# Expert rows gathered by token number, radial layers on parts of the TensorE array, and the last 226 counts summed in SBUF

## The chip, the cores and the metric

The kernel runs on one core of a Trainium2 chip. The metric is the device time of that core in microseconds (us), one launch from begin to end, lower is better. The engines are named as the profile names them: PE (TensorE, the matrix engine), DVE (VectorE), ACT (ScalarE), POOL (GpSimd), SP (SyncE, which here only issues DMAs). PSUM, where PE writes, has eight banks of 512 fp32 columns.

## The reference, cut to what matters

The input `x` has 1250 rows of 512. Four blocks follow one another, each added to its own input:

```python
x = x + gnn(layernorm(x), edge_attr_4, edge_attr_8, edges)   # 40000 edges, dst is sorted
x = x + grouped_moe(layernorm(x))
x = x + gat2(layernorm(x), edges)                            # two attention layers, 4 heads x 256, and a linear
x = x + expert_choice(layernorm(x))                          # 16 experts
```

The change touches the first two:

```python
# gnn: x0 = up-projected scalars (n,128), x1 = vectors (n,128,3)
h = edge_feats                                   # (edges, 8)
for W in (W1, W2, W3):                           # 8x64, 64x64, 64x64
    h = c * silu(h @ W / sqrt(len(W)))
w1, w2, w3, w4 = split(h @ W4 / 8, 4)            # 64 -> 4 x 128
p1 = w1 * x0[src] * y0;      p2 = w2 * x0[src] * y1
p3 = w3 * x1[src] * y0;      p4 = w4 * sum(x1[src] * y1) / sqrt(3)
msg = segment_sum(p1, p4, p2, p3 by dst);  out = lin(msg) / 10

# grouped_moe: 4 groups of 8 experts, every token keeps 2 groups, and in each of them 2 experts
gw = topk_gate(x @ wg_group, 2);  z = layernorm(x)
for g: iw = topk_gate(z @ wg_inner[g], 2)
       y_g = layernorm(z + sum_e iw[e] * (relu(z @ W1[g,e] + b1) @ W2[g,e] + b2))
out = sum_g gw[g] * y_g
```

The attention layers need the same edges as a dense matrix of counts, 1250 by 1250: how many edges go from one node to another. It is made together with the segment sums of the first block.

## The kernel before, in words

**Stages.** By the trace, the first 87 us project `x` up to `xup_d` and order the edges; the edge stage runs from there to 735 us; a block stage (735 to 898) projects the sums out and gates the tokens; the 32 experts run from 898 to 1141; their rows are brought back and combined until 1240; the attention layers follow to about 1980 and the expert-choice block to the end.

**The edge stage** (`edge_sums`, from L464) walks over 45 steps. A step takes 4 columns (`CG`) x 2 halves (`GT`) x 128 edges. Its order is written out by hand in `beat(s)`: in one beat different steps are in different phases, and each engine runs its instructions in that order. In beat s, SP loads the edges of step s+4 (L516), DVE makes the indices of step s+3 (L521), POOL gathers the sender rows of step s+2 by eight indirect DMAs of 128 rows of 3300 bytes each (L528: 2 KB of scalars and vectors, then the sender's one-hot row of 1250 in fp8, from which the counts come), PE and ACT run the radial network of step s+2, weights and products are made for step s+1, and the sums are taken for step s.

PE's order in a beat: layer 0 (L545, four products of 128 columns each, with a `w1` that is mostly zeros), the weights of pair 0 (L581; a pair is one half of the edges in two columns, and its two products use 64 rows of the array each), part of the sums (L613, L620, four 32-column tiles side by side), layer 1 (L548, one product of 512 columns with a block-diagonal 128x128 `w2`, two 64x64 blocks on the diagonal and zeros elsewhere), sums, weights of pair 1, the counts of half 0 (L630: fp8, 1250 columns as 512 + 512 + 226, four columns of edges each), layer 2 (L548), weights of pair 2, sums, a transpose (L95), weights of pair 3, sums, the counts of half 1. ACT does the silus (L553), copies each pair's weights from PSUM to SBUF (L588, two copies a pair), copies sums and counts out (L640, L646) and scales what stays in PSUM for the next step (L643, L647: by 1 where a window of nodes goes on, by 0 where not; `going`). DVE multiplies weights and rows (L597 twice and L600 for each of four pairs), makes the one-hot matrices (L561, L564, L569), and in steps 4 to 27 also runs one of 24 slices of products for the attention layers (`att_products`, L1936). POOL also stores each step's 128 rows of 2274 fp32 to `sums_d` (L650, an indirect DMA). SP in addition writes zeros into `zs_d`, two blocks of 128 rows a step (issued in `side`, 88 DMAs of 256 KB).

The PSUM tiles are `pa` (sums, two banks), `pc` (counts, three), `pw` (weights, two buffers of one bank) and `pm` (layers, one). Node windows that need more than 45 steps, which no input of this shape here needs, lie behind an If.

**Grouped experts** (`grouped_moe`, from L836). Five blocks of two chunks of 125 tokens each: load the sums (`acc`) and project them out, layer norm, gating, a running count of tokens for each expert, and from it the slot of each of a token's four (expert, token) pairs. Each expert has 208 slots in `zs_d`. POOL adds the norm's bias to the row `z` (L1008), and eight indirect DMAs a block (L1043) write the 125 rows of 2 KB of a chunk to their slots, 40 in all; a pair beyond an expert's 208 slots goes to overflow tiles, which are behind an If that isn't taken with this input. SP's queue loads `acc` and `adj` rows and the first experts' weights; ACT's queue stores what becomes of `adj`. The order in this stage is made by a scheduler. Then each expert (L1132ff): SP loads its 208 rows as `zr` in one DMA of 416 KB, PE transposes them (L95) and multiplies with W1 and W2 (L1150, L1159), ACT applies relu (L1152), DVE adds the row (L1161), and ACT's queue stores `y` over the expert's slots. At the end the four rows of each token are gathered by `pair_slot` (L1215), and combined (L1256).

Of the kernel before, what the change touches and what calls it, by code (L numbers as in the profile page):

```python
# [53 lines left out]
MOE_ROWS = 32 * MOE_SL + MOE_NT * MOE_TS  # L54
# [406 lines left out]
def edge_sums(k, tables, sorted_d, xup_d, Ws, sums_d, zero, side):  # L461
# [14 lines left out]
    with ExitStack() as es:  # L476
# [7 lines left out]

        HC = CG // 2
        w1 = cp.tile([128, TT // 2, 128], F32, name="w1")
        nc.gpsimd.memset(w1, 0.0)
        w2 = cp.tile([128, 128], F32, name="w2")
        nc.gpsimd.memset(w2, 0.0)
        w3 = cp.tile([128, 128], F32, name="w3")  # L490
        nc.gpsimd.memset(w3, 0.0)
        w4 = cp.tile([128, 4 * 128], F32, name="w4")
        for u in range(2):
            half = slice(u * 64, (u + 1) * 64)
            for t in range(GT):
                for jp in range(HC):
                    r = ((2 * jp + u) * GT + t) * PW + 4
                    nc.sync.dma_start(w1[r:r + 8, t * HC + jp, half], Ws[0])
            nc.sync.dma_start(w2[half, half], Ws[1])
            nc.sync.dma_start(w3[half, half], Ws[2])  # L500
            nc.sync.dma_start(w4[half, :], Ws[3])
# [4 lines left out]
        pc = ps_a.tile([128, 3 * 512], F32, name="pc")  # L506
# [25 lines left out]
        def turn(s):  # L532
            pm = nets[s] = ps_m.tile([128, 512], F32, name="pm")
            k.transpose(pm[:, :128], pays[s].rearrange("p j t w -> p (j t w)"))

        def features(s):
            f = ep.tile([128, 128], F32, name="f")
            nc.scalar.copy(f, nets[s][:, :128])
            nets[s] = f

        def layer(s, i):
            pm = ps_m.tile([128, 512], F32, name="pm")
            if i == 0:
                for b in range(TT // 2):
                    nc.tensor.matmul(pm[:, b * 128:(b + 1) * 128], w1[:, b, :], nets[s], start=True,  # L545
                                     stop=True)
            else:
                nc.tensor.matmul(pm, (w2, w3)[i - 1], nets[s], start=True, stop=True)  # L548
            nets[s] = pm

        def silu(s, i):
            h = ep.tile([128, 512], F32, name=f"h{i}", bufs=1 + i // 2)
            nc.scalar.activation(h, nets[s], AF.Silu,  # L553
# [21 lines left out]
        def weights(s, t, jp):  # L575
            b = t * HC + jp
# [47 lines left out]

        def counts(s, t):
            eq = hots[s][0]
            for o in range(0, N, 512):
                e = min(N, o + 512)
                for j in range(CG):
                    nc.tensor.matmul(pc[j * WIN:(j + 1) * WIN, o:e], eq[:, j * GT + t, :],  # L630
                                     rows[s, t, j // 2][:, j % 2, D:].bitcast(FP8)[:, o:e],
                                     start=s == t == 0, stop=t == GT - 1, skip_group_check=True,
                                     tile_position=(0, j * WIN))
# [4 lines left out]
        def take_sums(s):  # L638
            outs[s] = ep.tile([128, SUMS], F32, name="out", bufs=3)
# [5 lines left out]
        def take_counts(s):  # L645
            nc.scalar.copy(outs[s][:, 1024:], pc[:, :N])  # L646
            nc.scalar.activation(pc[:, :N], pc[:, :N], AF.Copy, scale=going[:, s:s + 1])  # L647

        def store(s):
            st = nc.gpsimd.indirect_dma_start(  # L650
                out=sums_d, out_offset=bass.IndirectOffsetOnAxis(ap=sum_rows[:, s:s + 1], axis=0),
                in_=outs.pop(s), in_offset=None, bounds_check=CARRY + 127, oob_is_err=False)
# [14 lines left out]
        def carry_counts(s):  # L667
            if s == NS0 - 1:
                for o in range(0, N, 512):
                    e = min(N, o + 512)  # L670
                    nc.tensor.matmul(pc[:, o:e], carry_to, outs["carry"][:, 1024 + o:1024 + e],
                                     start=False, stop=True, skip_group_check=True)

# [13 lines left out]
        def beat(s):  # L687
# [31 lines left out]
            do(0, counts, 0)  # L719
            do(2, gather, 1)  # L720
# [12 lines left out]
            do(1, products, *pairs[3])  # L733
            do(0, sums, 1, 0, 3)
# [15 lines left out]
        with tc.If(rarely > 0):  # L750
            for s in range(NS0, NS):
# [8 lines left out]
                for t in range(GT):  # L760
# [7 lines left out]
                    counts(s, t)  # L768
                take_sums(s)
# [66 lines left out]
def grouped_moe(k, x, sums_d, nb_d, adjT_d, finish, zs_d, W_out0, W_out1, ln_g, ln_b, wg_group, wg_inner,  # L836
                W1, b1, W2, b2, gln_g, gln_b):

# [9 lines left out]
    SL, TS, NT = MOE_SL, MOE_TS, MOE_NT  # L848
# [5 lines left out]
    with ExitStack() as es:  # L854
        mp = es.enter_context(tc.tile_pool(name="moe", bufs=1, reuse_waits="tile"))
        pair_slot = mp.tile([P, NC, 4], I32, name="pair_slot")
        over_slot = mp.tile([P, NC, 4], I32, name="over_slot")
# [13 lines left out]
        teri = mp.tile([1, NT + 1], I32, name="teri")  # L871
        b1T = mp.tile([128, GX * HC], F32, name="b1T")
# [11 lines left out]
        with ExitStack() as s1:  # L884
# [42 lines left out]
            nc.vector.memset(ones, 1.0)  # L927
            ti = tp.tile([NT, 1], F32, name="ti")
# [42 lines left out]
            for blk in range(NB):  # L971
# [18 lines left out]
                for i in range(BC):  # L990
# [17 lines left out]
                    nc.gpsimd.tensor_tensor(z[:, c, :], z[:, c, :], lnb, op=ALU.add)  # L1008
                n = BC * (G + 1)
# [31 lines left out]
                for i in range(BC):  # L1041
                    for j in range(4):
                        st = nc.gpsimd.indirect_dma_start(  # L1043
                            out=zs_d, out_offset=bass.IndirectOffsetOnAxis(ap=p4i[:, i, j:j + 1], axis=0),
                            in_=z[:, blk * BC + i, :], in_offset=None, bounds_check=GX * SL - 1,
                            oob_is_err=False)
# [4 lines left out]
                if blk == 1:  # L1051
                    pre = [load(e) for e in range(6)]

# [36 lines left out]
            nc.vector.tensor_copy(pair_slot, p4)  # L1090
            p4o = tp.tile([P, NC, 4], F32, name="p4o")
            nc.vector.tensor_scalar(p4o, p4, float(GX * SL), FAR, op0=ALU.is_lt, op1=ALU.mult)
            nc.vector.tensor_tensor(p4o, p4o, p4, op=ALU.add)
            nc.vector.tensor_copy(over_slot, p4o)
# [949 lines left out]
```

## Time and profile before

| what | before |
|---|---|
| median of 9 runs | 2253.88 us (2247.28 to 2259.61) |
| the profiled execution | 2251.05 us, span 2249.3 |
| PE busy | 1939.4 us (86%) |
| DVE busy | 1384.9 us (62%) |
| ACT busy | 1023.2 us (45%) |
| POOL busy | 789.7 us (35%) |
| DMA | 421.75 MB, mean 188 GB/s |
| gathers L528 | 360, 433.3 us on POOL |
| `zs_d<-zero` | 88 DMAs of 256 KB |
| `zr<-zs_d` | 32 DMAs of 416 KB |

A busy share is a mean over stages which have different limits, so each stage is read by itself. A group of instructions is shown as line, engine, operation, output<-input, count, then busy time, mean ns of one, and the idle time of the engine just before them with what ended it. On a line of the timeline, the first number is the start in us, the second the duration; "x8" joins eight instructions that follow one another, and brackets hold the idle time before them and what ended it. "issue" is time in which the engine waited for nothing that the profile shows.

### The profile page before, as it was taken

The page shows a single profiled execution, that of the slowest core. Times are in us where ns is not written, and L with a number is a line of the kernel's source. Part 1 is how long each engine was busy: PE and PEld are TensorE (multiplying, and loading weights), DVE is VectorE, ACT ScalarE, POOL GpSimd, SP SyncE. Part 2 cuts the span into 40 slices and gives each one's busy share as a digit, 9 for nine tenths or more (in the row PEclk, how much of TensorE's full clock was granted, in tenths as well). Part 3 has the DMA queues.
Part 4 walks back from the last instruction along what each step waited for, and adds up shares of the span by engine and source line. Part 5 has one row for each costly group of instructions (what it writes and reads, how often), then busy time and mean ns, then how long its engine had stood idle before and what let it go on. Part 6 is the DMA issues. An engine that isn't in the chain of part 4 may idle for free. (4 is left out here: it accounts for less than half of the span.)

```text
span 2249.3 us, 31188 instructions
## 1 busy us (share of the span) xinstructions
PE 1939.4 (86%) x10813; PEld 1111.9 (49%) x10813; DVE 1384.9 (62%) x2944; ACT 1023.2 (45%) x1856; POOL 789.7 (35%) x671
## 2 busy tenths in 40 slices
PE   2599999999998463999979969999999999709996
PEld 2333333333333452766623447885457777505563
DVE  8289999998885455323347399875807777382000
ACT  2277777777775333211125347872216555101221
POOL 3377888887774266100045200000000001002342
PEclk9699999999999665999967989999999999858998
DMA  6799999999995876998644522205211221366752
GB/s 174 229 327 304 331 337 319 338 335 306 312 327 177 248 213 159 288 299 268 213 110 130 135 75 82 57 19 127 77 56 35 76 73 50 91 246 183 225 117 32
DMA packets 196586, 421.75 MB, mean 188 GB/s; under 512 B 66411, under 2 KB 86090, under 8 KB 192818
## 3 DMA queue, kind: packets, MB, share of 16 engines
q0 software_dynamic: 60416, 204.33, 28.8%
q1 hardware_dynamic: 116400, 183.36, 26.9%
q10 hardware_dynamic: 19599, 31.92, 4.5%
q8 instruction: 90, 1.47, 0.3%
q14 instruction: 81, 0.66, 0.1%
HBM read 326.25 MB, written 133.33 MB: 204 GB/s over the span
## 5 line engine op out<-in xcount | busy, mean ns | idle before, releaser
L528 POOL DMA_INDIRECT s<-xup_d,idx x360 | 433.3, 1204 | 130.9 <-issue 82.0
L1553 PE MATMUL po<-h,p 125*125 125x257 f32 x1600 | 363.8, 385 | 20.2 <-ACT p L1546 20.2
L597 DVE TENSOR_TENSOR m<-w,s 128x768 f32<-128x768 f32 x360 | 329.6, 956 | 51.2 <-ACT w L588 49.8
L1553 PEld LDWEIGHTS po<-h,p 125*125 125x125 f32 x1600 | 299.5, 190 | 71.8 <-ACT p L1546 23.1
L588 ACT COPY w<-pw 128x512 f32<-128x512 f32 x360 | 193.3, 589 | 95.1 <-PE pw L581 88.1
L1585 POOL TENSOR_TENSOR xc<-xc,fcb 125x512 f32<-125x512 f32 x10 | 18.2, 1839 | 610.8 <-DMA xc<-x_d 610.7
L1436 PE MATMUL ph<-w,xT 128*125 128x512 f32 x480 | 219.1, 614 | 2.0 <-DMA w<-in_L_gnn_W 0.8
L581 PE MATMUL pw<-w,h 64*128 64x512 f32 x720 | 205.9, 644 | 0.3 <-ACT w L588 0.2
L1532 ACT ACTIVATE q<-rr,ascol 125x250 f32<-125x250 f32 x400 | 165.9, 496 | 60.0 <-DVE p L1534 36.3
L1534 DVE SCALAR_TENSOR_TENSOR p<-rr,acol,q 125x250 f32<-125x250 f32 x400 | 171.0, 477 | 24.2 <-PE po L1553 14.7
L1436 PEld LDWEIGHTS ph<-w,xT 128*125 128x125 f32 x480 | 91.5, 194 | 123.4 <-issue 114.5
L620 PE MATMUL pa<-m,oh 128*32 128x256 f32 x2160 | 143.0, 383 | 0.0
L1488 DVE CUSTOM_DVE_ANT_0 junk<-row,nb 125x1250 bf16<-125x1250 f32 (+1 forms) x80 | 113.2, 1415 | 22.7 <-DMA row<-a_d 16.1
L600 DVE TENSOR_TENSOR m<-w,s 128x512 f32<-128x512 f32 x180 | 122.8, 682 | 0.0
L1538 DVE TENSOR_TENSOR p<-p,adjb 125x1250 f32<-125x1250 f32 x80 | 120.2, 1502 | 1.1
L1546 ACT ACTIVATE p<-p 125x1250 f32<-125x1250 f32 x80 | 98.0, 1240 | 46.5 <-DVE p L1538 34.8
L620 PEld LDWEIGHTS pa<-m,oh 128*32 128x32 f32 x2160 | 61.3, 109 | 117.0 <-issue 93.5
L1882 PE MATMUL po<-w,hT 128*78 128x512 f32 x256 | 115.7, 605 | 0.5 <-ACT hT L1874 0.5
L1159 PE MATMUL po<-w,hT 128*104 128x512 f32 x256 | 115.7, 595 | 0.0
L1161 DVE TENSOR_TENSOR y<-po,zr 104x512 f32<-104x512 f32 x64 | 44.2, 691 | 113.3 <-PE po L1159 111.1
L1152 ACT ACTIVATE hT<-ph,b1T 128x208 f32<-128x208 f32 x64 | 27.8, 434 | 185.0 <-PE ph L1150 171.8
L1827 DVE COPY xg<-px 128x624 f32<-128x624 f32 x16 | 12.9, 806 | 160.0 <-PE px L95 160.0
(461 smaller groups left out, 3100.7 us busy)
## 6 DMA issues: line engine op xcount, KB each, us to landing
w<-in_L_ffn_W SPq DMA_DIRECT2D x64, 512.0 KB
w<-in_L_ffn_w SPq DMA_DIRECT2D x32, 1024.0 KB
zs_d<-zero SPq DMA_DIRECT2D x88, 256.0 KB
zr<-zs_d SPq DMA_DIRECT2D x32, 416.0 KB
zs_d<-y ACTq DMA_DIRECT2D x32, 416.0 KB
adjb<-adjT_d SPq DMA_DIRECT2D x10, 1093.8 KB
rr<-r_d SPq DMA_DIRECT2D x8, 875.0 KB
attw<-in_L_gnn_W SPq DMA_DIRECT2D x12, 512.0 KB
```

The source lines that it names most:

```text
L528: nc.gpsimd.indirect_dma_start(out=sj[:, u], out_offset=None, in_=xup_d, in_offset=bass.IndirectOffsetOnAxis(ap=idxs[s][:, i:i + 1], axis=0))
L581: nc.tensor.matmul(pw, nets[s][half, b * 128:(b + 1) * 128], w4[half, :], start=True, stop=True)
L588: nc.scalar.copy(made[s, t, jp][2][:, u].rearrange("p a d -> p (a d)"), made[s, t, jp][u])
L597: nc.vector.tensor_tensor(m[:, u, :, 1:4, :], w[:, u, 2:4, None, :].to_broadcast(shape), v[:, u, None, 1:4, :].to_broadcast(shape), op=ALU ...
L600: nc.vector.tensor_tensor(m[:, :, :, 0, :], w[:, :, 0:2, :], v[:, :, 0:1, :].to_broadcast([128, 2, 2, 128]), op=ALU.mult)
L620: nc.tensor.matmul(pab[q, 1, a::3 - a, :] if a < 2 else pab[q, 1, 2:4, :], oh[:, i, 1 + a, :], ms[j][:, 1, 0:2 + a:1 + a, :], start=first ...
L1159: nc.tensor.matmul(po[:n], hT[:, hc, j * n:(j + 1) * n], w2[:, hc, :], start=hc == 0, stop=hc == HC - 1)
L1436: self.k.nc.tensor.matmul(ph, self.xT[:, i, c * P:(c + 1) * P], self.w[half][i], start=i == 0, stop=i == kin - 1)
L1532: nc.scalar.activation(q[:, i], rr[:, hd, :, 1, :], AF.Identity, bias=ascol[:, c, hd:hd + 1])
L1534: nc.vector.scalar_tensor_tensor(p[:, i], rr[:, hd, :, 0, :], acol[:, c, hd:hd + 1], q[:, i], op0=ALU.add, op1=ALU.max)
L1538: nc.vector.tensor_tensor(pf, pf, adjb[:, half * HS:(half + 1) * HS, :] .rearrange("p c n -> p (c n)"), op=ALU.add)
L1553: nc.tensor.matmul(po[q], p[:, i, q, :], h[:, c, hd, :], start=c == 0, stop=c == NC - 1)
```

## The change

In the edge stage:

- Layer 0 becomes four products of 64 rows: `w1` keeps both columns' weights of a pair, and rows 0 to 63 and 64 to 127 give different columns of the output. Layers 1 and 2 become four products of 64x64 on the four quarters of the array, 256 columns each; `w2` and `w3` hold two copies of the 64x64 matrix one above the other, with no zeros. The output `pm` has two banks now, of each 256 columns are used, and the halves of a layer's output lie in the order (pair of columns, half of edges).
- The counts' first 1024 columns stay in PSUM as before (`pc`, two banks). The last 226 are multiplied in a `pw` buffer right after the counts of half 0, for both halves (`counts_beyond`), copied by ACT into the step's `out` tile, and summed from step to step there: DVE adds the last step's 226 numbers times `going` (`add_beyond`).
- The zeros of `zs_d` are no longer written.

In the grouped experts:

- The rows `z` are stored once, in the tokens' order, to `z_d` (two SP DMAs a chunk, after L1008's addition). The 40 indirect DMAs now write a token's number (4 bytes) instead of its row to the slots, in a table `tok_d` of 64 x 104 that is filled before with numbers of valid tokens.
- After the last block, the table is loaded to SBUF, transposed by PE and copied by DVE to `token`. Each expert's rows come by two indirect gathers of 104 rows, issued by POOL (64 in all), in place of SP's one load.
- `zs_d` now holds the experts' outputs and the overflow tiles only, and shares its DRAM with `sums_d`. The second slot table `over_slot` is gone; `pair_slot` is worked out with one DVE operation less.

```diff
+        CUT = 1024
+        w1 = cp.tile([128, GT, 128], F32, name="w1")
-        w2 = cp.tile([128, 128], F32, name="w2")
-        nc.gpsimd.memset(w2, 0.0)
+        w2 = cp.tile([128, 64], F32, name="w2")
...
-                    nc.sync.dma_start(w1[r:r + 8, t * HC + jp, half], Ws[0])
-            nc.sync.dma_start(w2[half, half], Ws[1])
+                    nc.sync.dma_start(w1[r:r + 8, t, half], Ws[0])
+            nc.sync.dma_start(w2[half], Ws[1])
...
         def layer(s, i):
-            pm = ps_m.tile([128, 512], F32, name="pm")
-            if i == 0:
-                for b in range(TT // 2):
-                    nc.tensor.matmul(pm[:, b * 128:(b + 1) * 128], w1[:, b, :], nets[s], start=True,
-                                     stop=True)
-            else:
-                nc.tensor.matmul(pm, (w2, w3)[i - 1], nets[s], start=True, stop=True)
+            pm = ps_m.tile([128, 2, 512], F32, name="pm")
+            for b in range(2):
+                for r in range(2):
+                    q = slice(64 * r, 64 * r + 64)
+                    if i == 0:
+                        nc.tensor.matmul(pm[:, r, b * 128:(b + 1) * 128], w1[q, b, :], nets[s][q, :],
+                                         start=True, stop=True)
+                    else:
+                        v = b ^ r
+                        nc.tensor.matmul(pm[64 * v:64 * v + 64, r, :256], (w2, w3)[i - 1][q],
+                                         nets[s][q, 256 * v:256 * v + 256], start=True, stop=True,
+                                         tile_position=(64 * r, 64 * v))
...
+        def counts_beyond(s):
+            pw = ps_w.tile([128, 512], F32, name="pw")
+            for t in range(GT):
+                for j in range(CG):
+                    count(pw, s, t, j, CUT, N, t == 0)
+            outs[s] = ep.tile([128, SUMS], F32, name="out", bufs=3)
+            nc.scalar.copy(outs[s][:, 1024 + CUT:], pw[:, :N - CUT])
+
+        def add_beyond(s):
+            if s > 0:
+                last = outs[s][:, 1024 + CUT:]
+                nc.vector.scalar_tensor_tensor(last, outs[s - 1][:, 1024 + CUT:], going[:, s - 1:s], last,
+                                               op0=ALU.mult, op1=ALU.add)
...
         def take_counts(s):
-            nc.scalar.copy(outs[s][:, 1024:], pc[:, :N])
-            nc.scalar.activation(pc[:, :N], pc[:, :N], AF.Copy, scale=going[:, s:s + 1])
+            nc.scalar.copy(outs[s][:, 1024:1024 + CUT], pc)
+            nc.scalar.activation(pc, pc, AF.Copy, scale=going[:, s:s + 1])
...
             do(0, counts, 0)
+            do(0, counts_beyond)
...
             do(1, products, *pairs[3])
+            do(0, add_beyond)
...
+            number = tp.tile([P, NC], F32, name="number")
+            nc.gpsimd.iota(number, pattern=[[P, NC]], base=0, channel_multiplier=1,
+                           allow_small_or_imprecise_dtypes=True)
+            whose = tp.tile([2 * GX, HS], F32, name="whose")
+            nc.gpsimd.iota(whose, pattern=[[1, HS]], base=0, channel_multiplier=(N - HS) // (2 * GX),
+                           allow_small_or_imprecise_dtypes=True)
+            nc.sync.dma_start(tok_d, whose)
+            slot_d = tok_d.rearrange("e p -> (e p)")[:, None]
...
                     nc.gpsimd.tensor_tensor(z[:, c, :], z[:, c, :], lnb, op=ALU.add)
+                    spread(nc.sync, z_d[c * P:(c + 1) * P, :], z[:, c, :])
...
-                            out=zs_d, out_offset=bass.IndirectOffsetOnAxis(ap=p4i[:, i, j:j + 1], axis=0),
-                            in_=z[:, blk * BC + i, :], in_offset=None, bounds_check=GX * SL - 1,
-                            oob_is_err=False)
+                            out=slot_d, out_offset=bass.IndirectOffsetOnAxis(ap=p4i[:, i, j:j + 1], axis=0),
+                            in_=number[:, blk * BC + i:blk * BC + i + 1], in_offset=None,
+                            bounds_check=GX * SL - 1, oob_is_err=False)
...
+            nc.sync.dma_start(whose, tok_d)
+            pt = ps.tile([HS, 2 * GX], F32, name="pl")
+            k.transpose(pt, whose)
+            nc.vector.tensor_copy(token, pt)
...
             def rows(e):
                 zr = sp.tile([HS, 2, D], F32, name="zr", bufs=4)
-                nc.sync.dma_start(zr, zs_d[e * SL:(e + 1) * SL, :].rearrange("(j p) d -> p j d", p=HS))
+                for j in range(2):
+                    nc.gpsimd.indirect_dma_start(
+                        out=zr[:, j, :], out_offset=None, in_=z_d,
+                        in_offset=bass.IndirectOffsetOnAxis(ap=token[:, 2 * e + j:2 * e + j + 1], axis=0))
...
                 def side(s):
-
-                    for b in range(2 * s, min(2 * s + 2, MOE_ROWS // 128)):
-                        nc.sync.dma_start(zs_d[b * 128:(b + 1) * 128, :], zero[:, :D])
                     if 4 <= s < 4 + len(steps):
                         steps[s - 4]()
```

Instruction by instruction, the changed program differs in order in two more places. The store that fills `tok_d` stands in SP's queue between the first and the second load of `acc`, and waits for POOL's iota. The stores to `z_d` stand in SP's queue ahead of weight loads, and ahead of `acc` and `adj` loads of later blocks; those of chunks 4 and 5 are ahead of the `acc` loads of block 4. The first gathers of experts stand on POOL after the last scatter and one more operation; the later ones are issued two experts ahead.

## Prediction

> **What bounds the kernel now.** I read the slices first, then the windows of the edge stage, one beat of TensorE, then GpSimd and VectorE in the same stretch, last the block stage and the first expert. One slice is 56 us.
>
> ```profile
> PE   2599999999998463999979969999999999709996
> DVE  8289999998885455323347399875807777382000
> POOL 3377888887774266100045200000000001002342
> DMA  6799999999995876998644522205211221366752
> ```
>
> TensorE is at 9 in slices 3 to 12, the edge stage (87 to 735 us); there DVE is at 8 or 9, POOL at 7 or 8 and DMA at 9. Slices 13 to 16 (735 to 900) are the block stage: TensorE 4 to 6, DMA up to 9. Two windows of the edge stage, one with the GAT's `att_products` on DVE (steps 4 to 27), one without:
>
> ```profile
> 400.00:500.00 100.00, 100.00 (x858) 37.44 (x855) 93.97 (x177) 76.45 (x117) 79.87 (x67) 1.00 0.96 337
> 600.00:700.00 100.00, 99.61 (x862) 37.51 (x858) 84.40 (x116) 75.96 (x115) 80.08 (x66) 1.00 0.91 311
> ```
>
> After window and length come the busy times of PE, PEld, DVE, ACT, POOL, then TensorE's clock, DMA share, GB/s. TensorE is full in both, DVE nearly in the first. POOL's 80 is not slack: between its DMAs lie 0.30 us each time. The groups from 120 to 700 us:
>
> ```profile
> L528 POOL DMA_INDIRECT s<-xup_d,idx x337 | 407.1, 1208 | 102.7 <-issue 76.2 <-DMA s<-xup_d,idx 7.3 <-PE pm L95 7.3
> L650 POOL DMA_INDIRECT sums_d<-out,sum_rows x42 | 57.9, 1378 | 12.8 <-issue 8.8 <-ACT h L553 3.7 <-ACT w L588 0.3
> ```
>
> 407.1 + 102.7 + 57.9 + 12.8 = 580.5: the whole window. A beat is eight gathers and a store, 8 x (1.208 + 0.30) + 1.378 + 0.30 = 13.74 us. A beat of TensorE is as long (643.59 to 657.32). Some of its lines:
>
> ```profile
> 643.59 1.16 PE L545 MATMUL pm<-f,w 128*128 128x128 f32 x8
> 644.68 1.13 PE L581 MATMUL pw<-w,h 64*128 64x512 f32 x4
> 646.62 0.61 PE L620 MATMUL pa<-m,oh 128*32 128x256 f32 x8
> 647.16 1.13 PE L548 MATMUL pm<-h,w 128*128 128x512 f32 x2
> 648.22 1.07 PE L620 MATMUL pa<-m,oh 128*32 128x256 f32 x16
> 650.28 0.72 PE L630 MATMUL pc<-s,eq 128*32 128x512 fp8e4 x12
> ```
>
> From start to start, layer 0 (L545) takes 1.09, a later layer (L548) 1.06, a pair's weights (L581: two products on 64 rows, 512 columns each) 1.06, and four 32-column tiles of 256 columns (L620 x8) 0.54. So two products on row halves cost one full one, and four column tiles one quarter.
>
> POOL's 1.208 is no constant:
>
> ```profile
> 649.52 1.22 DVE L569 TENSOR_TENSOR oh<-eq,epay 128x1024 f32<-128x1024 fp8e4 x1
> 650.01 1.56 POOL L528 DMA_INDIRECT s<-xup_d,idx  x1 [0.30 <-DMA s<-xup_d,idx]
> 651.87 0.95 POOL L528 DMA_INDIRECT s<-xup_d,idx  x1 [0.30 <-issue]
> ...
> 92.17 0.95 POOL L528 DMA_INDIRECT s<-xup_d,idx  x1 [0.30 <-issue]
> ```
>
> The gather begun while L569 runs ends at 651.57, 0.83 us after L569 (650.74); the next takes 0.95, as all do up to 102 us, before DVE's products begin. Unstretched, a beat of POOL would be 8 x 1.25 + 1.3 = 11.3. The Trainium skill, page "SBUF — State Buffer", section "Who interferes with whom", says that a VectorE operation with two SBUF inputs and a GpSimd operation that reads SBUF hold each other off; 1.56 against 0.95 agrees, but the page infers that descriptor generation is spared under tensor_tensor, and these rows say it isn't. By the page the gathers would leave POOL's bound out of the sum, and the edge stage would gain 33 as in B below.
>
> **The change, edge stage.** (a) Layer 0 becomes four products of 64 rows and 128 columns, two at once: 2 x 128 columns deep, by L581's row half of L548's time, 1.09 to 0.55. Layers 1 and 2 become four 64x64 products of 256 columns; no row shows quarters. Bounds: 0.54 if four run at once (L620's tiles), 1.06 if only two do. I take 0.6, nearest to L620, which shows four tiles at once. Saving 0.54 + 2 x 0.46 = 1.46 a beat. The Trainium skill, page "TensorEngine Tiling (Array Packing)", section "Key Properties", says that a change of tiling mode drains the array, which speaks against quarters, a mode of their own; no row here isolates it. Layer 0 now has the mode of the weights next to it, so the changes of mode in a beat stay about as many, and by the page too the sum would not move much.
>
> (b) The 226 counts' products are the same in number, but go into a `pw` buffer behind `counts(0)`. That buffer comes free when pair 1's first ACT copy ends, about 650.9 by this beat's ACT copies (0.53 each from 650.38), and `counts(0)` without its third run ends at about 650.7: a new wait of 0.2. What stands behind it on PE is layer 2, whose silu feeds the next step's pair 0 half a beat later, so nothing else is late. ACT's copy is of the same columns as before, and the scaling of 226 columns goes: ACT (76%) is no bound. DVE gets `add_beyond`, 226 elements: L1936's 256 take 0.35 from start to start, so 0.31. It stands behind pair 3's products and only the store waits for it. PE's beat: 13.73 - 1.46 + 0.2 = 12.5 (13.9 if nothing of (a) is gained).
>
> (c) The zeros, 22.5 MB, leave SP's queue and the DMA rings. No engine waits on them: 0. If the DMA engines (share 0.91 to 0.96) held the gathers, this would be a gain inside the same sum.
>
> What the beat can use: in the 24 beats with `att_products`, DVE has one gap:
>
> ```profile
> 423.48 1.83 DVE L597 TENSOR_TENSOR m<-w,s 128x768 f32<-128x768 f32 x2 [0.60 <-ACT w L588]
> ```
>
> Its floor is 13.74 - 0.60 + 0.31 = 13.45: -0.29 x 24 = -7. In 20 others DVE needs 0.844 x 13.73 + 0.31 = 11.9, and the beat lies between PE's 12.5 and POOL's 13.74. POOL's stretch is made by DVE operations, which stay as many in a shorter beat, so it does not go by itself; but a stretch ends with the operation, so part of it moves with DVE. I take the middle, 13.1: -0.63 x 20 = -12.6. Edge stage -20, bounds 0 and -33.
>
> **The change, grouped experts.** Tail and first expert:
>
> ```profile
> 886.62 1.19 POOL L1043 DMA_INDIRECT zs_d<-z,p4i  x1 [0.30 <-issue]
> 893.75 1.68 SPq L1132 DMA_DIRECT2D zr<-zs_d  x4
> 898.68 1.62 PE L95 MATMUL pz<-ident,zr 104*128 104x104 f32 x8 [4.47 <-DMA zr<-zs_d]
> ...
> 1147.92 1.28 POOL L1215 DMA_INDIRECT ya<-zs_d,pair_slot  x1 [0.92 <-issue]
> 1153.78 0.75 DVE L1256 SCALAR_TENSOR_TENSOR m<-ya,iw,pm 125x512 f32<-125x512 f32 x1 [12.30 <-DMA ya<-zs_d,pair_slot]
> ```
>
> The chain from the end of the last scatter to the first expert was 898.68 - 887.81 = 10.9. Now: the scatter's landing 4 (0 to 5.9, the time to 893.75), the numbers' load 2.5 (2 to 4.9, that of `zr`), transpose and copy 0.8, two gathers 3.0, their landing 4.6 (1149.20 to 1153.78): 14.9, so +4 (-0.5 to +8.3). A scatter of 4-byte numbers has no row of its own: POOL issues it as before (1.19), and its landing has the bounds just given.
> The 40 scatters carried 256 KB each, 10 MB; now 2.56 MB go to `z_d`: 7.5 MB less, 25 us of DMA at 300 GB/s in a stage with share 0.9 to 1.0 between 755 and 805. Only part lies on the path, such as ACT's `adjt` held 11.81 us at 825 by an issue: -4 (-15 to 0). Against it, 20 `z_d` stores wait in SP's queue for POOL's additions L1008, with weights and later `acc` and `adj` loads behind them, and the pre-fill of `tok_d` stands between the first and second `acc` load until POOL's iota, about 742.4, some 2.5 us; that one is hidden, since PE waits until 752.10 for ACT's `at`. I take +2 (0 to 15).
>
> Experts: 64 gathers on POOL, 3.0 of each expert's 7.1 us, two experts ahead, on an engine nearly idle there; if that cover went, 3.0 an expert. SP's weight loads lose `zr` ahead of them; PE is busy 16.45 of 20 in 985 to 1005: -2 (-3.5 to 0). Together 4 - 4 + 2 - 2 = 0.
>
> **Sum.** 2251.05 (the profiled execution, span 2249.3) - 20 = 2231; the median of the runs shown is 2.8 higher: 2234.
>
> **Rivals.** B: POOL yields and TensorE sets the beat: -7 - 20 x 1.23 = -32, and the block stage gains 10 of its 15 from fewer bytes: 2212. For it: unstretched, POOL needs 11.3. Against: no gap on POOL in 580 us. C: POOL's gathers hold the beat at 13.74, nothing of (a) and (b) shows: 2253. For it: 13.74 on both sides is an odd coincidence unless one paces the other. Against: DVE's gap ends on ACT and PE, not on a gather. That the quarters save nothing (1.06) belongs here: 13.9, also about 2254. D, the slower side: SP's queue in the block stage. The `acc` loads that SP starts at 785.51 stand behind `z_d` stores whose additions POOL ends at 803.7 (L1008 from 801.16, behind eight scatters): 18.2 late, and with the chain at its upper 8.3, +26 against the edge stage's -20: 2260. It decides once the block stage and the chain lose more than 20. For it: SP is in order and POOL is booked with scatters. Against: PE's waits in that stretch end mostly on ACT and DVE.
>
> **How the numbers follow.** The forecast 0.45, B 0.27, C 0.15, D 0.13. The range is 2208 to 2259: it holds the forecast's case, nearly all of B and C, and leaves out most of D; the forecast's own range is 2222 to 2246. A measurement of this kernel tells 0.2% (2249.4 to 2258.4) from no change. Faster: the forecast, B and a little of C, 0.74; same, most of C and some of D, 0.12; slower 0.14.
>
> **What would show it.** Layer slots near 0.55 to 0.6 in TensorE's beat; DVE's 0.60 gap gone in beats with L1936; 13.1 us between stores in later beats, POOL without gaps but with shorter gathers; first expert some 15 us after the last scatter; stage 735 to 898 about as long. Wrong, if layers keep 1.06, if POOL shows idle time (B), or if `acc` loads come late (D).

## The result and the profile after

The changed kernel takes 2266.39 us (median of 20 runs, 2256.48 to 2273.38) where the kernel before takes 2250.94 (62 runs): a ratio of 1.0067, 95% interval 1.0056 to 1.0078. It is slower by 0.7%; 2234 was forecast, with a range that ended at 2259. The two profiled executions differ by 15.4 us (span 2264.7 against 2249.3), and five marks of the traces divide that up:

| from, to | before | after | difference | forecast |
|---|---|---|---|---|
| start to the last store of the edge stage (L650, L671) | 731.28 | 725.37 | -5.9 | -20 |
| to the end of the last scatter (L1043, L1083) | 156.5 | 171.3 | +14.7 | -2 |
| to the first expert's transposes (pz) | 10.9 | 15.6 | +4.8 | +4 |
| to the end of the experts (the first transpose of mix) | 243.4 | 243.6 | +0.2 | -2 |
| to the end of the span | 1107.2 | 1108.8 | +1.6 | 0 |

The slices of the changed kernel, with fewer bytes to move (391 MB against 422) and a lower DMA share in the edge stage and behind it:

```profile
PE   2599999999985543999979969999999999709996
POOL 3487777778883255532246200000000001002342
DMA  6788998988885682898735432204211221366752
```

Two windows of its edge stage, the columns as in the prediction (PE, PEld, DVE, ACT, POOL, clock, DMA share, GB/s):

```profile
400.00:500.00 100.00, 93.05 (x971) 33.84 (x971) 98.17 (x186) 77.14 (x129) 79.61 (x67) 1.00 0.89 291
600.00:700.00 100.00, 89.28 (x867) 32.73 (x865) 83.45 (x118) 68.59 (x114) 80.81 (x64) 1.00 0.83 261
```

TensorE is no longer full: it has 7 to 11 us in 100 to spare. In the first window DVE is now full (98.17), in the second nothing seems to be, except POOL, which has no gap between its DMAs. Its groups from 120 to 690 us show that:

```profile
L530 POOL DMA_INDIRECT s<-xup_d,idx x332 | 403.7, 1216 | 101.2 <-issue 71.3 <-DMA s<-xup_d,idx 9.4 <-PE pa L627 6.1
L671 POOL DMA_INDIRECT long_d<-out,sum_rows x41 | 53.8, 1313 | 12.5 <-issue 10.1 <-ACT h L560 1.2 <-ACT w L595 0.9
```

403.7 + 101.2 + 53.8 + 12.5 = 571.2, again the whole stretch, and a gather still has a mean of 1.216 us (1.208 before). From store to store the beats with attention products (14th to 28th store) are 13.44 us long on average, 13.87 before (medians 13.44 and 13.73); those without them (28th to 42nd) are 14.13, 13.76 before (medians 13.90 and 13.73), and they are uneven, from 12.48 to 17.52. So the first kind of beat gained as forecast and the second lost. What DVE's products waited for where no attention products run (520 to 680 us), first before, then after:

```profile
L597 DVE TENSOR_TENSOR m<-w,s 128x768 f32<-128x768 f32 x94 | 86.9, 965 | 23.5 <-ACT w L588 23.5
...
L604 DVE TENSOR_TENSOR m<-w,s 128x768 f32<-128x768 f32 x92 | 86.2, 956 | 23.8 <-DMA s<-xup_d,idx 19.4 <-ACT w L595 2.7 <-ACT out L667 1.0
```

Before, they waited for weights, which come from TensorE by way of ACT; after, for gathered rows.

TensorE's own part of the change is there. Some lines of its timeline:

```profile
602.04 0.66 PE L553 MATMUL pm<-h,w 64*64 64x256 f32 x8
602.63 1.07 PE L627 MATMUL pa<-m,oh 128*32 128x256 f32 x16
...
605.83 0.38 PE L633 MATMUL pw<-s,eq 128*32 128x226 fp8e4 x8 [0.36 <-ACT w L595]
...
641.80 0.72 PE L549 MATMUL pm<-f,w 64*128 64x128 f32 x8
642.35 1.03 PE L588 MATMUL pw<-w,h 64*128 64x512 f32 x4
```

From start to start a later layer takes 0.59 (1.06 before) and layer 0 takes 0.55 (1.09 before): four quarters run at once. The wait for a free `pw` buffer (0.36 here, 0.12 in 38 of 44 steps, 1.26 at most) is the one that the counts' move brings. TensorE's largest wait in this stage is another, which the prediction did not have: from 120 to 690 us it waits 27.5 us for ACT to scale the sums in `pa`, and before not at all.

```profile
L620 PE MATMUL pa<-m,oh 128*32 128x512 f32 x672 | 89.5, 605 | 27.5 <-ACT pa L664 27.5
```

And this is POOL beside DVE in a beat without attention products:

```profile
641.39 0.96 DVE L604 TENSOR_TENSOR m<-w,s 128x768 f32<-128x768 f32 x1 [0.43 <-DMA s<-xup_d,idx]
641.49 1.69 POOL L530 DMA_INDIRECT s<-xup_d,idx  x1 [0.30 <-DMA s<-xup_d,idx]
...
643.40 0.96 DVE L604 TENSOR_TENSOR m<-w,s 128x768 f32<-128x768 f32 x1 [1.05 <-DMA s<-xup_d,idx]
643.48 1.71 POOL L530 DMA_INDIRECT s<-xup_d,idx  x1 [0.30 <-PE pw L588]
```

A product that has waited for a gather's rows starts at 641.39, and the next gather but a moment later. The product ends at 642.35 and the gather 0.83 us after it, at 643.18, the same 0.83 as in the prediction's reading. The next product waits for rows again and starts at 643.40, just ahead of the next gather. Here the two run in step, 2.0 us a gather. Eight gathers of 1.39 to 2.47 us and a store made the beat that ended at 651.05 17.5 us long, the longest of these beats.

In the block stage, SP's queue of the changed kernel:

```profile
736.31 0.49 SPq L965 DMA_DIRECT2D tok_d<-whose  x1
737.38 9.09 SPq L79 DMA_DIRECT2D acc<-long_d  x7
746.70 3.50 SPq L79 DMA_DIRECT2D adj<-long_d  x4
...
775.63 3.68 SPq L79 DMA_DIRECT2D z_d<-z  x4
...
787.79 3.84 SPq L79 DMA_DIRECT2D z_d<-z  x4
...
796.47 2.14 SPq L79 DMA_DIRECT2D acc<-long_d  x4
```

and what TensorE waited for in the same stretch:

```profile
755.39 0.34 PE L97 MATMUL pl<-ident,b1r 64*128 64x64 f32 x1 [5.73 <-DMA b1r<-in_L_ffn_b]
...
811.46 1.90 PE L97 MATMUL pt<-ident,acc 125*128 125x125 f32 x8 [15.03 <-DMA acc<-long_d]
...
900.10 0.32 PE L97 MATMUL pl<-ident,whose 64*104 64x64 f32 x1 [20.83 <-DMA whose<-tok_d]
```

The kernel before waited 1.28 us for `b1r` and not at all for the third block's `acc`, which SP started there at 775.07:

```profile
755.07 0.34 PE L95 MATMUL pl<-ident,b1r 64*128 64x64 f32 x1 [1.28 <-DMA b1r<-in_L_ffn_b]
...
775.07 2.98 SPq L77 DMA_DIRECT2D acc<-sums_d  x4
```

Two losses are to be seen. First, the filling of `tok_d` holds seven `acc` loads and the `adj` loads behind it by some 3 us, and the small loads of ACT's queue, `b1r` last, land late: ACT issues `b1r` at 746.71, beside the `adj` loads, and TensorE has it 8.7 us later; before, it was issued at 750.91, ahead of them, and there 4.2 us later. That the delayed loads are what slows `b1r` is inferred from this order. TensorE begins on `b1r` 30.0 us after the edge stage's last store (23.8 before), and the first addition of L1047 comes 49.0 us after it (41.0 before). Second, two groups of `z_d` stores, each waiting for an addition on POOL, stand ahead of the `acc` loads, so that these begin at 796.47 and TensorE has nothing to do for 15.0 us.

### The profile page after: what moved, and what is told of

Its sections match the earlier page's. It is cut to its first block, busy times and chain, and to the rows that moved or that the text cites. A ratio compares the mean times of both kernels' runs of the same rounds, so it can differ in the third digit from the quotient of the medians.

```text
span 2264.7 us, 32357 instructions
## 1 busy us (share of the span) xinstructions
PE 1893.2 (84%) x11354; PEld 1086.4 (48%) x11354; DVE 1400.8 (62%) x2989; ACT 1015.5 (45%) x1901; POOL 851.6 (38%) x735
## 5 line engine op out<-in xcount | busy, mean ns | idle before, releaser
L588 PE MATMUL pw<-w,h 64*128 64x512 f32 x720 | 213.5, 639 | 3.3 <-ACT w L595 2.4
L1582 DVE SCALAR_TENSOR_TENSOR p<-rr,acol,q 125x250 f32<-125x250 f32 x400 | 170.0, 475 | 24.1 <-PE po L1601 14.7
L620 PE MATMUL pa<-m,oh 128*32 128x512 f32 x720 | 96.6, 609 | 30.9 <-ACT pa L664 30.9
```

The source lines that it names most:

```text
L588: nc.tensor.matmul(pw, nets[s][half, b * 128:(b + 1) * 128], w4[half, :], start=True, stop=True)
L1582: nc.vector.scalar_tensor_tensor(p[:, i], rr[:, hd, :, 0, :], acol[:, c, hd:hd + 1], q[:, i], op0=ALU.add, op1=ALU.max)
```

## The experiments

The first four kernels ran beside a kernel before of 2249 us. The others ran in four groups (e5 to e8, e9 to e12, e13 to e16, e17 and e18) beside one of 2289 to 2291, with mean beats of 14.4 to 15.4 us in every variant that makes all its gathers; their ratios are compared only among themselves, and best within a group. Times "after the last store" are from the edge stage's last store in each kernel's own trace.

### Each half of the change alone (e1, e2)

e1 is the kernel before with the changed `edge_sums`, e2 the changed kernel with `edge_sums` of before:

```diff
-def edge_sums(...):   # of the one kernel
+def edge_sums(...):   # of the other
```

> The kernel before with the edge stage of the changed one alone (quarter layers, last 226 counts in SBUF), the zeros kept and the experts as before. Theory: the edge stage ends about 6 us earlier, as its last store does in the changed kernel's trace (725.4 against 731.3), with beats of 13.45 where the attention products run and 14.1 after them; nothing else moves, so 0.997 of before. Rival (the zeros' transfers cost the gathers something): beats after step 28 longer than 14.1 and no gain or a loss, 1.000 or more.

> The changed kernel with the edge stage of before: no zeros, experts' rows by token number. Theory: the whole loss is here, in the block stage (+15) and in the chain from the last scatter to the first expert (+5): 1.009 of before, beats of 13.73 throughout. Rival (the two parts cost each other, the loss in the block stage comes with the earlier end of the edge stage): 1.003 or less.

e1: 2240.18 against 2249.26, ratio 0.9965 (0.9947 to 0.9983). e2: 2270.03, ratio 1.0090 (1.0068 to 1.0113). Both are as expected, and 0.9965 x 1.0090 = 1.0055, about the whole change. So the loss is all in the grouped experts, and the kernel with the changed edge stage alone gains a third of a per cent. Its trace is 11.6 us shorter than that of before: 4.9 of them in the edge stage, and 3.6 in the block stage, whose code is that of before. That is how far marks differ without a change: eight traces with the block stage of before took 153.0 to 156.5 us from the last store to the last scatter, eight with the changed one 167.6 to 171.3. By these the stage's loss is 11 to 18 us, and the 14.7 above is one pair. In e1, with the zeros back and DMA share 0.90 to 0.96, the beats are 13.45 with attention products and 14.2 without, as in the changed kernel: the zeros cost the gathers nothing that shows. e1 is faster than both kernels.

### What sets the beat (e4, e7)

```diff
         def gather(s, t):
             for jp in range(HC):
+                if t:
+                    rows[s, t, jp] = rows[s, 0, jp]
+                    continue
```

e4 has this in the changed kernel, e7 in the kernel before.

> The changed kernel with four of a step's eight gathers: the second half of the edges uses the first half's rows, so the sums and counts are of other rows. Theory (POOL's gathers, stretched by DVE, set the beat where no attention products run): those beats fall from 14.1 to PE's 12.5 to 12.7, beats with attention products stay at 13.45, the kernel is 22 to 28 us shorter than the changed one. Rival (the hand-over of weights through two PSUM buffers, with the counts' extra use of one, sets it): beats stay at 13.8 to 14.1.

> The kernel before with four of a step's eight gathers, the second half of the edges on the first half's rows. Theory (there PE set the beat at 13.73 and POOL only kept step, stretched by DVE's operations): beats stay at 13.73 and the time within 4 us of before. Rival (POOL set the beat before, too): beats fall to 13.1 or less, over 15 us.

e4: 2237.55, 29 us below the changed kernel's median (22 to 28 expected); beats 13.42 with attention products and 12.75 without (medians). e7: 2243.40, and its beats are 13.73 (median), those of the kernel before. That is as expected; the time is not within 4 us of before, but 7.5 below the 2250.94 of above and 48 below the 2291 of the kernel before in its own group. So in that group the full set of gathers costs the kernel before 48 us; no trace of it from that group shows where. POOL's stores in e4's timeline:

```profile
568.44 1.06 POOL L674 DMA_INDIRECT long_d<-out,sum_rows  x1 [5.19 <-ACT out L670]
...
581.19 1.80 POOL L674 DMA_INDIRECT long_d<-out,sum_rows  x1 [5.20 <-ACT out L670]
```

POOL now waits 5.2 us in each beat, and a beat is 581.19 - 568.44 = 12.75. With the gathers out of the way the two kernels differ by what the change does on TensorE: 13.73 before, 12.75 after (13.42 where DVE is full). Before, TensorE set the beat; after, POOL's gathers do wherever DVE is not full. DVE's products then no longer wait for rows (e4, 520 to 680 us):

```profile
L607 DVE TENSOR_TENSOR m<-w,s 128x768 f32<-128x768 f32 x102 | 93.0, 953 | 10.7 <-PE pa L630 8.1 <-PE pc L636 1.1 <-ACT w L598 0.2
```

ACT's scaling of `pa`, TensorE's largest wait above, is the same work in e4, and there it costs 0.25 us in a beat of 12.75, so it is not what makes the long beats. e4 takes away half of the issue time and half of the rows' bytes at once; that the issue is what counts is read from POOL's rows in the changed kernel, where nothing but the 0.30 lies between two DMAs.

### SP's queue in the block stage (e3, e5, e6, e9, e10)

```diff
-                    spread(nc.sync, z_d[c * P:(c + 1) * P, :], z[:, c, :])
+                    spread(nc.gpsimd, z_d[c * P:(c + 1) * P, :], z[:, c, :])
...
-            nc.sync.dma_start(tok_d, whose)
+            nc.gpsimd.dma_start(tok_d, whose)
...
-        nc.gpsimd.tensor_tensor(t[:, r:r + 2], t[:, r:r + 2], none, op=ALU.subtract)
+        (less or nc.gpsimd).tensor_tensor(t[:, r:r + 2], t[:, r:r + 2], none, op=ALU.subtract)
```

e3 has the first of these, e5 the second, e6 and e10 all three (the last with `less` as `nc.vector` for the blocks beside the experts); e9 is the changed kernel itself.

> The changed kernel with the 20 stores of rows to z_d issued by POOL, which makes the rows, in place of SP. Theory (SP's stores wait for POOL's additions and hold the loads of acc behind them): PE's wait of 15.0 us for acc at 811 goes, the last scatter comes 8 to 14 us earlier, 0.995 of the changed kernel, about 1.001 of before. Rival (the scatters of single numbers or the crowded DMA engines at the start of the stage make it longer): within 3 us of the changed kernel, 1.005 or more of before.

> The changed kernel with the first filling of tok_d issued by POOL, right where its numbers are made, in place of SP between the first and the second acc load. Theory (SP's wait there moves seven acc loads and the adj loads by 3 us, so that ACT's small loads land behind them: PE waits 5.7 us for b1r and the first addition of L1047 comes 49 us after the last store of the edge stage, 41 before): the addition comes at 41 to 43, PE's wait for b1r falls below 2 us, the kernel is 5 to 8 us shorter than the changed one, 1.003 to 1.005 of before. Rival (b1r lands late for another reason, such as the shared DRAM of sums and expert rows): 49 stays, no change.

> The changed kernel with three moves at once: z_d's stores and the filling of tok_d issued by POOL, and the subtractions of adjacency that run beside the experts done by DVE, so that none stands ahead of POOL's first gathers. Theory: 6 us for the first (as measured), 5 to 8 for the second, 4 for the third (the first gather stood 5 us behind the copy of the numbers): last scatter 157 to 160 us after the last store of the edge stage, first expert 11 to 12 after it, 15 to 18 us shorter than the changed kernel, 0.998 to 1.001 of before. Rival (waits are only passed on to ACT's and DVE's chains of the blocks): 6 us or less.

> The changed kernel itself, beside the next three on one chip, since the last four kernels ran where the kernel before took 2291 us and its gathers landed later. Theory and rival alike: 1.005 to 1.009 of before where before takes about 2250; on a chip with late gathers more.

> The kernel of e6 beside the changed one. In e6's trace the last scatter ended 157 us after the edge stage's last store (changed kernel 171, before 157) and the first expert began 173 after it (187, 167). Theory: 13 to 15 us shorter than the changed kernel here, 1.000 to 1.002 of before. Rival (the moves lose in the experts or later what they win here): less than 6 us.

| us after the last store | first L1047 | last scatter's end | first expert |
|---|---|---|---|
| before | 41.0 | 156.5 | 167.4 |
| changed | 49.0 | 171.3 | 186.9 |
| e2, grouped experts alone | 47.7 | 169.8 | 185.2 |
| e3, z_d by POOL | 49.0 | 164.9 | 180.3 |
| e5, tok_d by POOL | 43.0 | 166.2 | 181.8 |
| e6, all three | 40.0 | 157.3 | 173.2 |
| e9, changed, again | 47.9 | 170.3 | 186.0 |
| e10, all three, again | 40.5 | 159.8 | 175.7 |

In e3 SP starts the third block's loads 53 us after the last store (71 in the changed kernel, 44 before), and TensorE's wait of 15 us is gone:

```profile
783.26 1.94 SPq L79 DMA_DIRECT2D acc<-long_d  x4
```

The stage is 6.4 us shorter (171.3 to 164.9), where 8 to 14 were expected. As a time it hardly shows: 2259.52, ratio 1.0056 (1.0038 to 1.0074) against 1.0067, which by itself is the rival's forecast. e5 has the first addition back at 43.0 and the stage 5.1 us shorter; both stages are below the 167.6 to 171.3 of the changed code. But in e5 TensorE still waits 4.58 us for `b1r`, where less than 2 was expected, so the part of `b1r` in the delay is not shown. (e13, with the block stage of before, waits 4.44 for it, e6 and e10 1.2 and 1.4.) e5's time, 1.0186 of a kernel before of 2291, can't be set against e3's, and against e9 (1.0131, in the next group) it is no gain, so e5 tells by its trace alone. Together the moves give most of the stage back: e10 takes 2306.21 against e9's 2320.01 in the same group, 13.8 us less, as expected; 1.0072 (1.0047 to 1.0097) against 1.0131 (1.0101 to 1.0161) of before, where 1.000 to 1.002 was expected. By the traces 10.5 us of it lie in the block stage. e6 missed its forecast as a time, 1.0186, the same as e5 beside it, with mean beats of 15.3 in the edge stage; its block stage has the marks of e10.

The third move gave nothing. In e10 the first gather starts as soon as the numbers are there, but TensorE does the expert's transposes no earlier, 15.9 us after the last scatter (15.6 in the changed kernel):

```profile
939.70 1.03 POOL L1178 DMA_INDIRECT zr<-z_d,token  x1 [4.40 <-DVE token L1097]
...
950.17 1.20 PE L97 MATMUL pt<-ident,adj 125*125 125x125 f32 x4 [1.34 <-ACT adjt L859]
951.17 0.38 PE L97 MATMUL pz<-ident,zr 104*128 104x104 f32 x1
952.71 1.20 PE L97 MATMUL pt<-ident,adj 125*125 125x125 f32 x4 [1.16 <-ACT adjt L859]
```

The transposes of the expert's rows (pz) stand on TensorE behind those of `adj`, each of which waits for ACT. The wait has only moved from POOL to TensorE.

### Quarters and counts apart, and DVE's work moved (e8, e11, e14, e18; e12, e15; e13; e16, e17)

Three variants more, each run at least twice. The first is the changed kernel with the layers of before and the 226 counts still in SBUF; the second is e1 with the attention products in halves over 41 steps; the third is e1 with them 16 steps later. e13 is e1 again.

```diff
-                nc.tensor.matmul(pm[64 * v:64 * v + 64, r, :256], (w2, w3)[i - 1][q], ...)
+                nc.tensor.matmul(pm, (w2, w3)[i - 1], nets[s], start=True, stop=True)
...
-                    if 4 <= s < 4 + len(steps):
-                        steps[s - 4]()
+                    if s >= 4:
+                        for i in range((s - 4) * len(steps) // 41, (s - 3) * len(steps) // 41):
+                            steps[i]()
...
-                    if 4 <= s < 4 + len(steps):
-                        steps[s - 4]()
+                    if 20 <= s < 20 + len(steps):
+                        steps[s - 20]()
```

> The changed kernel with the layers of before (full products, one bank), the last 226 counts still summed in SBUF. Theory: PE's beat is 13.73 plus the new wait of 0.2, 13.9, so beats with attention products rise from 13.45 to 13.9 and the others stay near 14: 8 to 12 us longer than the changed kernel, 1.011 of before. Rival (the quarters bring nothing, DVE and POOL set both kinds of beat): the changed kernel's time.

> The kernel of e8 (layers as before, 226 counts in SBUF) beside the changed one. Theory: beats with attention products 13.9 in place of 13.45, 8 to 12 us longer than the changed kernel. Rival (the quarters bring nothing): the changed kernel's time.

> The kernel of e8 and e11, where before takes about 2250. Theory: beats with attention products 13.9 in place of the changed kernel's 13.45, the others 13.9 to 14.1: 1.010 to 1.012 of before against the changed kernel's 1.0067. Rival (the quarters bring nothing anywhere): 1.0067 and beats of 13.45.

> e1 (the changed edge stage in the kernel before) with the attention products in 48 halves over steps 4 to 44 in place of 24 slices over steps 4 to 27; the work is the same. DVE's floor is then 11.9 + 48/41 x 0.93 = 13.0 in every beat. Theory (a beat is long where DVE has nothing else to do and runs right behind the gathers, so that each product holds the next gather; with DVE full, gathers run ahead): beats of 13.1 to 13.5 throughout, 10 to 20 us shorter than e1, 0.988 to 0.993 of before. Rival (POOL needs 13.7 to 14.1 unless DVE needs 13.45): beats of 13.7 to 14.1 throughout, up to 10 us longer than e1, 0.997 to 1.001 of before.

> e1 again, beside the next three on one chip. Theory: 0.995 to 0.998 of before where before takes about 2250. Where gathers land late (before near 2290) no forecast is made.

> The kernel of e12 beside e1's. Theory (DVE with work in every beat keeps behind the gathers): 10 to 20 us shorter than e13, beats of 13.1 to 13.5. Rival: beats of 13.7 to 14.1, the time of e13 or up to 10 us more.

> e1 with the attention products in steps 20 to 43 in place of 4 to 27: the same work, 16 steps later. Theory (without them DVE runs right behind the gathers and holds them): beats before step 20 become 13.9 to 14.3 and those of steps 20 to 43 are 13.45; the time is that of e13 within 5 us. Rival (the later beats are long for another reason, such as what is stored or loaded there): beats before step 20 fall to 12.5 to 13.2 or stay at 13.45, those after step 28 stay near 14.

> e16's kernel once more, for a chip where the kernel before takes about 2250. Theory: beats before step 20 13.9 to 14.3, those of steps 20 to 43 13.45, the time 0.995 to 0.999 of before. Rival (long beats belong to their place): beats before step 20 12.5 to 13.45, those after step 28 near 14. Where before takes 2290: as e16.

> e14's kernel once more, for the same reason. Theory: beats with attention products 13.9, 1.010 to 1.012 of before. Rival (the quarters bring nothing): 13.45, 1.0067. Where before takes 2290: as e8, e11 and e14, 1.010 to 1.012, no different from the changed kernel there.

| run | ratio to before | interval | mean beat, stores 5 to 20 | 28 to 41 |
|---|---|---|---|---|
| e9, changed | 1.0131 | 1.0101 to 1.0161 | 14.82 | 14.42 |
| e8, full layers | 1.0116 | 1.0090 to 1.0142 | 14.82 | 14.49 |
| e11, e14, e18, full layers | 1.0096, 1.0113, 1.0110 | 1.0067 to 1.0134 | 14.42 to 14.55 | 14.43 to 14.48 |
| e13, as e1 | 1.0014 | 0.9995 to 1.0033 | 14.46 | 14.36 |
| e12, e15, spread | 1.0057, 1.0071 | 1.0035 to 1.0094 | 14.44 to 14.50 | 14.5 to 14.9 |
| e16, e17, late | 1.0033, 1.0014 | 0.9996 to 1.0053 | 14.85, 14.48 | 14.47, 14.60 |

For the beats no forecast of a theory came true, and no rival is shown by that: beside a kernel before of 2289 to 2291 no variant has mean beats of 13.45, e13 included, whose code had them in e1. Some times came out as forecast (1.010 to 1.012 for e8, e14 and e18; e16 within 5 us of e13; e15, 9 us longer than e13, by its rival), but not by the beats that were to bring them, so they count as luck. Spreading the products brought no short beats and was 0.4 to 0.6% longer than e13, so as a remedy it failed there. Full layers were as fast as quarters in these groups (1.010 to 1.012 against 1.013; beside e9, e11 was 8.9 us shorter where 8 to 12 longer were expected, though the intervals overlap). So what the quarters are worth as a time was not measured apart from the counts. Whether the long beats of the changed kernel come from DVE having less to do, as the lines at 641 to 645 us suggest, or from something else about these steps, was not settled; e16 and e17, which were to tell, have long beats with and without the products. What is settled is that four gathers fewer remove them (e4).

## Why the prediction was wrong

**The edge stage, -20 forecast, -5.9 measured.** The working on TensorE held: layer slots 0.55 and 0.59 where 0.55 and 0.6 were taken, 12.75 in e4 where a beat of 12.5 was worked out, and a wait for `pw` of 0.2 that is mostly 0.12. What is missing is in e4 mostly the wait for ACT's scaling of `pa`, 0.25 a beat, which the prediction put at nothing ("ACT (76%) is no bound"). DVE's floor held to a hundredth: 13.45 forecast, 13.44 measured in the beats with attention products, with `add_beyond` at 0.37 where 0.31 was taken. The Trainium skill, page "TensorEngine Tiling (Array Packing)", section "Key Properties", says that a change of tiling mode drains the array; in these slots of 0.55 and 0.59 no such cost shows. The step that failed is "I take the middle, 13.1" for the 20 other beats. They became longer, 14.13: a gather there takes 1.252 us on average, 1.222 before. The prediction had seen that POOL had no gap in 580 us, and had rival C for it, but bounded it by 13.74, as if a stretch that DVE makes could only stay or shrink. DVE's products now wait for rows in place of weights (19.4 of 23.8 us), and in the lines at 641 to 645 us each starts with the next gather and holds it; that this is why the stretch grew is argued from these lines, and no run isolates it. C was nearest to the truth in these beats, and even it was too hopeful there. (Two slips in the sums change nothing: the zeros are 88 x 128 rows of 2 KB, 23.1 MB and not 22.5, and the gain without POOL's bound is 7 + 25 = 32, as in B, not 33.)

**Grouped experts, 0 forecast, about +21 measured** (+14.7, +4.8, +0.2 and +1.6). Two steps failed. "That one is hidden, since PE waits until 752.10 for ACT's `at`" looked at one consumer of the delayed loads; the delay came through all the same, 8 us at the first addition (49.0 against 41.0; e5 gives back 6 of it, and 5.1 of the stage). By which load it came is open: `b1r`, which lands late, is the likely one. And "+2 (0 to 15)" for the stores in SP's queue took the lower end; e3 puts their part at 6.4. Rival D named this mechanism, at the fourth and fifth block instead of the third, and had the sign; it got 0.13. The -4 for fewer bytes doesn't show: the DMA share between 745 and 855 us fell from 0.87 to 0.67, and yet e6 and e10, with both kinds of store off SP's queue, have a stage of 157.3 and 159.8 us, no shorter than the 153.0 to 156.5 of before's code.

**The chain from the last scatter, +4 forecast, +4.8 measured**, right as a sum by luck and not in its terms. Landing and the numbers' load took 3.5 us (896.64 to 900.10), not 6.5; two gathers and their landing 4.6 (907.67 to 912.28), not 7.6; but between the numbers' transpose and the first gather lay 7.6 and not 0.8, because the gathers stood behind L860, which waited 9.60 us for ACT:

```profile
906.24 1.24 POOL L860 TENSOR_TENSOR adjt<-adjt,none 125x500 f32<-125x500 f32 x1 [9.60 <-ACT adjt L859]
907.67 1.03 POOL L1178 DMA_INDIRECT zr<-z_d,token  x1 [0.19 <-DVE p4o L1136]
```

The experts themselves gained nothing (+0.2, -2 forecast).

## What to carry to other kernels

Where two engines both fill a beat, the one that isn't shortened sets the next bound, and if it is stretched by a third engine's work that bound may rise, as here from 13.76 to 14.13; halving its load, as e4 does, shows in one run how much there is to win. A store that waits for a result goes onto the queue of the engine that makes the result, not in front of loads on an in-order queue. A delay is hidden only if every consumer behind it in the queue has slack; one consumer that waits for something else anyway, as TensorE did for `at`, doesn't show that.

## What was not expected of the hardware

A gather issued by POOL and a product on DVE that waits for gathered rows can fall into step, as from 641 to 645 us, at 2.0 us a gather, where a gather alone takes 0.95 + 0.30. In the groups beside a kernel before of 2289 to 2291 us, engines often waited for nothing that the profile shows (TensorE 21.6 us for the last counts' products in e13, from 120 to 690 us, none in e1, the same code), the mean beat of every variant with all its gathers was 14.4 to 15.4, and with half of them (e7) 13.73 to 13.78; what makes such waits stayed open.
